# Layer 1 by list schedules with real and imaginary parts on the partitions, and the convolution passes' stores by Pool

## The chip, the cores and the metric

The kernel runs on one core of a Trainium2 chip. The metric is the device time of one execution in microseconds (us), of which the median of several is taken. The core has five engines: TensorE (PE; its weight loads are shown apart as PEld), VectorE (DVE), ScalarE (ACT), GpSimd (POOL) and SyncE (SP), which only issues DMAs here. ACT and POOL can issue DMAs too. All DMAs share 16 DMA engines. Everything is float32.

## The reference

A batch x of 8 images with 32 channels of 256x256 goes through four layers, each `x = x + layer(gn(x))`, where `gn` normalises groups of two channels. The change is in layers 0 and 1.

```python
# layer 0: two hyperbolic 3x3 convolutions
out = _hconv(x, w1, b1);  out = _hrelu(_hbn(out, g1, beta1))
out = _hconv(out, w2, b2); out = _hrelu(_hbn(out, g2, beta2))
# _hconv: u = logmap0(x); y = conv3x3(u) + b; project(expmap0(y))
# logmap0, expmap0 and project scale each pixel by a function of its norm over the channels
# layer 1 (xs = every second row and column; p, q of 4 poles; i, k channels)
alpha = fft2(xs)
inv1 = 1 / (wp1 - lam1);  inv2 = 1 / (wp2 - lam2)
t1   = einsum('biox,oikp->bikpx', alpha, inv1)
res1 = einsum('bikpx,xikq,ikpq->bkpq', t1, inv2, res)
e1 = exp(wp1 * y);  e2 = exp(wp2 * x)          # complex
tmp = einsum('abpq,bipz->abqiz', res1, e1)
x1  = real(einsum('abqiz,biqx->aizx', tmp, e2)) / (Sx * Sy)
```

Layer 2 (mixing in windows) and layer 3 (a binary pattern) are the longer half of the kernel and are not touched.

## The kernel before

Seven stages follow one another. Intermediate images lie in DRAM (`v1`, `v2`, `x1`, `x2`, `x3`).

- **first_pass** (L519) and **second_pass** (L613): the two convolutions. An image lies on the partitions as 4 bands of rows x 32 channels (`pad`, two buffers), and is worked on in 8 units of 8 rows. For each image first come the norms: squares on ACT (`square`), four 128x32 matmuls per unit that add them over channels (`norms`, L309), the scale factor on small tiles (`artanh_over`, `cut`), then 16 times a pair of matmuls that spreads the factor over the channels into PSUM tile `q`, of which there is one buffer (L348), and a DVE product into `pad` (L588 in the first pass). Then each unit is convolved (`convolution`, L373): 144 matmuls of 32x32 weights (L391), two ACT copies of PSUM into `u` (L405), squares, the norm (L416), `cut`, two spreads (L429) with products on DVE (L434), statistics, and four stores of 256 KB each to `v` (L451) on the SP queue. `u` has two buffers. The first pass also loads `pad` by 16 DMAs per image on the SP queue (L549) and takes group statistics of the image (`stats`, `combine`, with a `pow` on POOL).
- **third_pass** (L683): the end of layer 0, writes `x1`. Its stores are issued by POOL (L810).
- **laplace_forward** (L862): a setup computes `1/(wp - lam)` for both axes, times the DFT matrices, into `g1`, `g2a`, `g2b` (8 blocks of 1024 columns: DVE work, one square on POOL, 64 matmuls, copies). Then, for each of the 32 input channels: load `xs`; two DVE operations normalise it into `xn`; 8 matmuls of 256 columns into `pz`; a copy to `zs` shared by ACT and DVE; 64 matmuls of 128x32 weights and 8 columns into `pt` (L963); and four DVE operations that add `pt` times the residues to `acc`. The result `res` goes to DRAM (`scratch`).
- **laplace_inverse** (L983): `scratch` is read back (`r`), and with a mask becomes block diagonal weights `bd`. For each block of 4 channels, two complex exponentials are made from angles on DVE and sines on ACT. For each channel, `xt` (2 MB) is loaded; for each of 8 images: two matmuls of 128x128 weights and 512 columns accumulate into `pu` (L1059, from `ea` and `eb`: one complex product takes both, since only the 32x4 pairs of output channel and pole lie on the partitions), ACT copies to `us` (L1067), four matmuls of 128x128 and 256 columns into `po` (L1071), DVE adds to `xt` (L1074) and takes statistics (L1077). `xt` is stored on the SP queue.
- **row_norms** (L1082): group means and variances from those statistics. `rsqrt_col` (L233) takes a `pow` on POOL over 256 columns (L241).
- **mixing** (L1338) and **binary_pattern** (L1619): layers 2 and 3.

The order of work in both convolution passes is set by `Plan` (L120). Every step is given with its engine, an assumed duration (`took`), an assumed time until its result is there (`lag`), and how much earlier than its job it ranks (`lead`). `issue` simulates engines that take the ready step of the lowest rank, counts free buffers, and emits the instructions in that order. The hardware then runs each engine's list in order. `conv_pass` (L505) mixes the units of image b with the preparation of image b+1. Before the change, `laplace_forward` and `laplace_inverse` are plain loops that the tile framework orders by dependencies.

Of the kernel before, what the change touches and what calls it, by code (L numbers as in the profile page):

```python
# [32 lines left out]
P = 128  # L33
NB = 8
# [229 lines left out]
def flat(ap):  # L264
    return ap.rearrange("p a b -> p (a b)")
# [5 lines left out]
class Strip:  # L271
# [101 lines left out]
    def convolution(self, pad, b, k, w):  # L373
# [27 lines left out]
        u = Buf(self.work, [P, 4, FD], "u", 2)  # L401
# [19 lines left out]
        s = self.narrow("cut", 2)  # L421
# [26 lines left out]
        def store():  # L448
            for j in range(4):
                at = k * UN + j * FD  # L450
                nc.sync.dma_start(dst[:, :, at : at + FD], u[32 * j : 32 * j + 32])  # L451

        plan.add("SP", 1.2, store, [u], lag=6.0)
# [12 lines left out]
    def artanh_over(self, pn):  # L466

        nc, plan = self.cx.nc, self.plan
        ln, w, p, z = (self.narrow(x) for x in ("ln", "w", "p", "z"))
        f = self.narrow("f", 2)  # L470
# [6 lines left out]
        ts(ln, pn, NORM_EPS**2, None, ALU.max)  # L477
        act(ln, ln, AF.Ln)
        act(w, ln, AF.Exp, scale=0.5)
        act(f, ln, AF.Exp, scale=-0.5)  # L480
# [132 lines left out]
def second_pass(cx, v1, sb, v2):  # L613
# [5 lines left out]
    with (  # L619
# [9 lines left out]
        def prepare(b):  # L629
# [29 lines left out]
            def narrow():  # L659
                f = strip.narrow("f", 2)  # L660
                strip.cut(f, pn)
                times = lambda rows, pf: nc.vector.tensor_tensor(rows, rows, pf, ALU.mult)
                later.extend(strip.factors(pad, f, times))
# [198 lines left out]
def laplace_forward(cx, x1, norms, scratch):  # L862

    nc = cx.nc
    KP = NC * M1
    with (
        cx.tc.tile_pool(name="g", bufs=1) as gp,
        cx.tc.tile_pool(name="wl", bufs=2) as work,
    ):


        g1 = gp.tile([P, NC, 2, KP], F32, name="g1", tag="g1")
        g2a = gp.tile([P, NC * NC, 2, M2], F32, name="g2a", tag="g2a")
        g2b = gp.tile([P, NC * NC, 2, M2], F32, name="g2b", tag="g2b")
        cosm, sinm, nsinm = (cx.keep(n, gp) for n in ("dft_cos", "dft_sin", "dft_nsin"))
        freq = cx.keep("dft_freq", gp)
        with cx.tc.tile_pool(name="pg", bufs=2, space=PSUM) as psum:
            for axis, grid in ((0, "L1_conv_x_grid"), (1, "L1_conv_t_grid")):
                zg = gp.tile([P, 3], F32, name="zg", tag=f"zg{axis}")
                nc.sync.dma_start(zg[:], cx.ins[grid][:, 0:3].to_broadcast([P, 3]))  # L880
                lam = gp.tile([P, 1], F32, name="lam", tag=f"lam{axis}")
                nc.vector.tensor_tensor(lam[:], zg[:, 2:3], zg[:, 0:1], ALU.subtract)
                nc.vector.reciprocal(lam[:], lam[:])
                nc.vector.tensor_tensor(lam[:], lam[:], freq[:], ALU.mult)
                BL = 2 * FD
                for blk in range(NC * KP // BL):
                    cols = slice(blk * BL, (blk + 1) * BL)
                    wr = work.tile([P, BL], F32, name="wr", tag="wr")
                    wi = work.tile([P, BL], F32, name="wi", tag="wi")
                    for t, part in ((wr, "r"), (wi, "i")):  # L890
                        src = cx.ins[f"L1_conv_wp{axis + 1}{part}"].rearrange("(o i) k p -> o (i k p)", o=1)
                        nc.sync.dma_start(t[:], src[:, cols].to_broadcast([P, BL]))
                    den = work.tile([P, BL], F32, name="den", tag="den")
                    tmp = work.tile([P, BL], F32, name="tmp", tag="tmp")
                    nc.vector.tensor_scalar(wi[:], wi[:], lam[:], None, ALU.subtract)
                    nc.vector.tensor_tensor(den[:], wr[:], wr[:], ALU.mult)
                    nc.gpsimd.tensor_tensor(tmp[:], wi[:], wi[:], ALU.mult)
                    nc.vector.tensor_tensor(den[:], den[:], tmp[:], ALU.add)
                    nc.vector.reciprocal(den[:], den[:])
                    nc.vector.tensor_tensor(wr[:], wr[:], den[:], ALU.mult)  # L900
                    nc.vector.scalar_tensor_tensor(wi[:], wi[:], -1.0, den[:], ALU.mult, ALU.mult)
                    for h in range(BL // FD):
                        hc = slice(h * FD, (h + 1) * FD)
                        pg = psum.tile([P, 2, FD], F32, name="pg", tag="pg")
                        nc.tensor.matmul(pg[:, 0, :], cosm[:], wr[:, hc], start=True, stop=False)
                        nc.tensor.matmul(pg[:, 0, :], sinm[:], wi[:, hc], start=False, stop=True)
                        nc.tensor.matmul(pg[:, 1, :], cosm[:], wi[:, hc], start=True, stop=False)
                        nc.tensor.matmul(pg[:, 1, :], nsinm[:], wr[:, hc], start=False, stop=True)
                        lo = blk * BL + h * FD
                        if axis == 0:  # L910
                            i0 = lo // KP
                            for c in range(2):
                                nc.vector.tensor_copy(
                                    g1[:, i0 : i0 + FD // KP, c, :],
                                    pg[:, c, :].rearrange("p (i k) -> p i k", k=KP),
                                )
                        else:
                            k = slice(lo // M2, (lo + FD) // M2)
                            re, im = (pg[:, c, :].rearrange("p (k q) -> p k q", q=M2) for c in range(2))
                            nc.vector.tensor_copy(g2a[:, k, 0, :], re)  # L920
                            nc.vector.tensor_copy(g2a[:, k, 1, :], im)
                            nc.scalar.copy(g2b[:, k, 1, :], re)
                            nc.scalar.mul(g2b[:, k, 0, :], im, -1.0)

        acc = gp.tile([NB * M1, 2, NC, 2, M2], F32, name="racc", tag="racc")
        nc.vector.memset(acc[:], 0.0)
        with (
            cx.tc.tile_pool(name="pz", bufs=1, space=PSUM) as psz,
            cx.tc.tile_pool(name="pt", bufs=2, space=PSUM) as pst,
        ):  # L930
            for i in range(NC):
                xs = work.tile([P, NB, W], F32, name="xs", tag="xs")
                nc.sync.dma_start(xs[:], x1[:, i].rearrange("b (y t) w -> t y b w", t=2)[0])
                rr = work.tile([NB * M1, 2, NC * 2 * M2], F32, name="rr", tag="rr")
                nc.sync.dma_start(rr[:], cx.ins["res"][:, i])
                xn = work.tile([P, NB, SUB], F32, name="xn", tag="xn")
                nc.vector.tensor_tensor(
                    xn[:], xs[:, :, 0:W:2], norms[:, :, 0, i : i + 1].to_broadcast([P, NB, SUB]), ALU.mult
                )
                nc.vector.tensor_tensor(  # L940
                    xn[:], xn[:], norms[:, :, 1, i : i + 1].to_broadcast([P, NB, SUB]), ALU.add
                )
                pz = psz.tile([P, NB, 2 * KP], F32, name="pz", tag="pz")
                for b in range(NB):
                    nc.tensor.matmul(
                        pz[:, b, :],
                        xn[:, b, :],
                        g1[:, i].rearrange("p c k -> p (c k)"),
                        start=True,
                        stop=True,  # L950
                    )
                zs = work.tile([P, 2, NC, NB, M1], F32, name="zs", tag="zs")
                half = NB // 2
                zt = zs.rearrange("p c k b m -> p b (c k) m")
                zf = pz.rearrange("p b (c m) -> p b c m", m=M1)
                nc.scalar.copy(zt[:, :half], zf[:, :half])
                nc.vector.tensor_copy(zt[:, half:], zf[:, half:])
                pt = pst.tile([NB * M1, NC * 2 * M2], F32, name="pt", tag="pt")
                for k in range(NC):
                    o = pt[:, k * 2 * M2 : (k + 1) * 2 * M2]  # L960
                    ik = i * NC + k
                    for c, g2 in enumerate((g2a, g2b)):
                        nc.tensor.matmul(  # L963
                            o,
                            zs[:, c, k].rearrange("p b m -> p (b m)"),
                            g2[:, ik].rearrange("p c q -> p (c q)"),
                            start=c == 0,
                            stop=c == 1,
                        )
                for c in range(2):  # L970
# [8 lines left out]
        for c in range(2):  # L979
            nc.sync.dma_start(scratch[c], res[:, c].rearrange("p k q -> p (k q)"))  # L980


def laplace_inverse(cx, x1, scratch, x2):  # L983

    nc = cx.nc
    KP = NC * M1
    BL = 4
# [886 lines left out]
```

## Time and profile before

| what | value |
|---|---|
| time, median of 3 runs | 14024.65 us (14023.85 to 14066.98) |
| the profiled execution: its own time | 14021.73 us |
| its span | 14020.0 us |
| PE / PEld / DVE busy | 10705.7 / 4220.3 / 8731.4 us |
| ACT / POOL busy | 7714.0 / 166.6 us |
| DMA | 1834.96 MB, mean 131 GB/s |

All readings are from the one profiled execution. A line of a group reads: source line, engine, operation, output<-input with shapes, count, then busy us and mean ns of one, then idle time of that engine just before such instructions and what ended most of it. In tables by stretch, each engine's busy time is followed by its instruction count; PEclk is the granted TensorE clock (1 is full). "issue" as a releaser is time in which the engine waited for nothing that the profile shows.

### The profile page before, as it was taken

What the parts mean: (1) busy time and instruction counts of PE and PEld (TensorE: products, weight loads), DVE (VectorE), ACT (ScalarE), POOL (GpSimd) and SP (SyncE); (2) the same over time, 40 slices, a digit from 0 to 9 for tenths busy, and PEclk for the clock granted to TensorE, in tenths of its full rate; (3) what the DMA queues carried; (4) which work ended last, traced back from release to release, by engine and by line L of the source; (5) the groups of instructions that cost most, each with busy time, mean ns of one, the idle gap of its engine ahead of it and who ended that gap; (6) DMA issues with size and microseconds to landing.
All of it is one profiled execution on the core that took longest, in us unless ns stands there. A gap on an engine that the chain in (4) does not pass through costs nothing.

```text
span 14020.0 us, 359842 instructions
## 1 busy us (share of the span) xinstructions
PE 10705.7 (76%) x165700; PEld 4220.3 (30%) x165700; DVE 8731.4 (62%) x7524; ACT 7714.0 (55%) x6456; POOL 166.6 (1%) x340
## 2 busy tenths in 40 slices
PE   5877899974447899367887878878788788987666
PEld 1222233320016566122332323323232233322222
DVE  3544343344564554256787878878787788887555
ACT  2332444443310222366877778777777778775555
POOL 0000000000000000100000000000000000000000
PEclk8887889975557899588998989989899899998777
DMA  5344333345642244455566556655665565553444
GB/s 95 75 91 91 95 100 103 102 116 187 196 148 77 95 149 149 109 148 144 143 150 155 145 145 150 153 147 137 156 150 151 141 151 147 132 132 98 129 126 126
DMA packets 1562774, 1834.96 MB, mean 131 GB/s; under 512 B 634352, under 2 KB 1279536, under 8 KB 1495728
## 3 DMA queue, kind: packets, MB, share of 16 engines
q1 hardware_dynamic: 1527472, 1744.72, 47.9%
q0 software_dynamic: 33792, 67.21, 1.5%
q8 instruction: 1301, 21.32, 0.6%
q14 instruction: 209, 1.71, 0.0%
HBM read 1140.39 MB, written 671.12 MB: 129 GB/s over the span
## 4 chain that ended last, share of the span: by engine, by line
PE 15%; DVE 14%; DMA 11%; ACT 10%; SPq 5%; issue 4%; DVEq 0%; ACTq 0%; POOL 0%; POOLq 0%
PE acc L1276 10%; DVE en L1304 8%; DMA raw<-x 4%; ACT e L1250 4%; DMA yt<-y 3%; DMA xt<-x 3%; SPq L1381 2%; DVE xc L1237 2%; PE q L1196 2%; SPq L1701 1%; DVE s L1682 1%; ACT e L1294 1%; ACT xc L1213 1%; PE q L1221 1%; SPq L1384 1%
## 5 line engine op out<-in xcount | busy, mean ns | idle before, releaser
L1276 PE MATMUL acc<-en,k_kw 32*32 32x512 f32 x49152 | 2164.5, 626 | 492.1 <-DVE en L1304 454.3
L1304 DVE SCALAR_TENSOR_TENSOR en<-e,en 128x2048 f32<-128x2048 f32 x1024 | 2343.7, 2289 | 210.6 <-PE acc L1276 155.7
L1250 ACT ACTIVATE e<-xc,off 128x2048 f32<-128x2048 f32 x768 | 1515.0, 2008 | 569.2 <-DVE xc L1237 489.2
L1304 DVE SCALAR_TENSOR_TENSOR en<-e 128x2048 f32<-128x2048 f32 x512 | 1170.8, 2287 | 348.4 <-ACT e L1294 190.8
L1276 PEld LDWEIGHTS acc<-en,k_kw 32*32 32x32 f32 x49152 | 710.4, 105 | 1482.9 <-DVE en L1304 1009.7
L1276 PE MATMUL acc<-e,k_kw 32*32 32x512 f32 x16384 | 1036.2, 673 | 104.0 <-ACT e L1294 35.5
L1237 DVE TENSOR_TENSOR xc<-xc,q 128x1024 f32<-128x1024 f32 x640 | 751.0, 1215 | 489.8 <-PE q L1230 489.5
L1294 ACT ACTIVATE e<-e 128x2048 f32<-128x2048 f32 x512 | 970.3, 1924 | 1.5
L1682 DVE TENSOR_TENSOR s<-raw 128x2313 f32<-128x2313 f32 (+2 forms) x256 | 627.7, 2495 | 478.3 <-DMA raw<-x 478.3
L1668 PE MATMUL acc<-s,mats 32*32 32x512 f32 x16384 | 697.9, 728 | 231.9 <-ACT s L1685 223.1
L1685 ACT ACTIVATE s<-s,vecs 128x2313 f32<-128x2313 f32 (+2 forms) x256 | 554.4, 2170 | 553.7 <-DVE s L1682 553.7
L405 ACT ACTIVATE u<-acc,k_vec 128x1024 f32<-128x1024 f32 x256 | 270.8, 1108 | 1062.3 <-DMA v<-u 694.0
L391 PE MATMUL acc<-pad,wb 32*32 32x512 f32 x18432 | 736.9, 649 | 141.1 <-issue 131.8
L1213 ACT ACTIVATE lsq<-q 128x1024 f32<-128x1024 f32 x512 | 526.6, 1028 | 530.6 <-PE q L1196 468.1
L434 DVE TENSOR_TENSOR u<-u,q 128x1024 f32<-128x1024 f32 x256 | 312.4, 1220 | 738.6 <-PE q L429 547.7
L391 PE MATMUL acc<-pad,k_cw 32*32 32x512 f32 x18432 | 736.6, 625 | 15.7 <-ACT u L405 10.8
L711 PE MATMUL n<-sq,k_gather 128*32 128x512 f32 x1024 | 243.7, 1045 | 439.6 <-ACT sq L729 438.2
L1276 PE MATMUL acc<-sg,k_kws 128*32 128x512 f32 x4096 | 504.5, 636 | 47.9 <-DVE sg L1335 40.6
L1196 PE MATMUL q<-yt,k_center 32*32 32x512 f32 x4096 | 313.2, 722 | 284.3 <-DMA yt<-y 227.8
L1213 ACT ACTIVATE xc<-q 128x1024 f32<-128x1024 f32 x512 | 529.3, 1034 | 0.0
L348 PE MATMUL q<-f,k_spread 32*128 32x512 f32 x1024 | 392.8, 853 | 173.2 <-DVE pad L588 93.0
L1071 PE MATMUL po<-ea,us 128*128 128x256 f32 x2048 | 506.5, 391 | 1.2 <-ACT us L1067 1.2
(291 smaller groups left out, 15967.4 us busy)
## 6 DMA issues: line engine op xcount, KB each, us to landing
v<-u SPq DMA_DIRECT2D x512, 256.0 KB
xt<-x SPq DMA_DIRECT2D x128, 1024.0 KB
pad<-v SPq DMA_DIRECT2D x64, 1024.0 KB
v<-v SPq DMA_DIRECT2D x64, 1024.0 KB
xt<-in_x SPq DMA_DIRECT2D x64, 1024.0 KB
x<-xt POOLq DMA_DIRECT2D x64, 1024.0 KB, 38.8
xt<-x SPq DMA_DIRECT2D x32, 2048.0 KB
x<-xt SPq DMA_DIRECT2D x32, 2048.0 KB
```

The source lines that it names most:

```text
L391: nc.tensor.matmul(acc[i // 2][32 * j : 32 * j + 32, i % 2, :], w[rows, tap, :], pad[rows, r : r + 2, dx : dx + W], start=tap == 0, stop=t ...
L1071: nc.tensor.matmul(po[:, t, :], us[:, c, t:W:2], ex[:, j, c, :], start=c == 0, stop=c == 1)
L1196: nc.tensor.matmul(pc[32 * j : 32 * j + 32, t, :], center[rows, :], src[rows, j * FD : (j + 1) * FD], start=True, stop=True,)
L1213: lambda pc=pc, h=h, fn=fn, out=out: nc.scalar.activation(half(out, h), flat(pc.get()), fn, bias=bias),
L1237: lambda pr=pr, h=h: nc.vector.tensor_tensor(half(xc, h), half(xc, h), flat(pr.get()), ALU.mult),
L1250: nc.scalar.activation(es[d][:], xs[:].rearrange("p i n -> p (i n)"), AF.Exp if exp else AF.Square, bias=kan.off[:, d : d + 1], scale=2.0 ...
L1276: nc.tensor.matmul(acc[bank][32 * to : 32 * to + 32, :], w[rows, out] if w.shape[-1] == P else w[rows, :], rhs[rows, cols] if rhs.shape[-1 ...
L1294: plan.add("ACT", 1.91, lambda: nc.scalar.activation(es[d][:], es[d][:], AF.Exp, scale=-1.0), [], [es[d]])
L1304: lambda: nc.vector.scalar_tensor_tensor(n[:], es[-1][:], BIG, prev[:], ALU.min, ALU.mult),
L1668: nc.tensor.matmul(acc[i][32 * j : 32 * j + 32, :], mats[part, m, part], rhs[part, 2 * j : 2 * j + 2, :], start=m == 0, stop=m == len(weig ...
L1682: nc.vector.tensor_tensor(d, raw[:, r0 + dy : R + 1 + dy, c0 + dx : c1 + dx], raw[:, r0 : R + 1, c0:c1], ALU.subtract)
L1685: nc.scalar.activation(d, d, AF.Sigmoid, scale=vecs[:, 0, b : b + 1])
```

## The change

Four parts.

**Convolution passes.** `u` gets a third buffer, and the stores of `v` go from the SP queue to the POOL queue; the plan gets 4.0 and 12.0 us for them in place of 1.2 and 6.0. To make room, the narrow tiles `cut` and `f` go from two buffers to one, and `ln` and `w` share one tile.

```diff
-        u = Buf(self.work, [P, 4, FD], "u", 2)
+        u = Buf(self.work, [P, 4, FD], "u", 3)
...
-        s = self.narrow("cut", 2)
+        s = self.narrow("cut")
...
-                nc.sync.dma_start(dst[:, :, at : at + FD], u[32 * j : 32 * j + 32])
-
-        plan.add("SP", 1.2, store, [u], lag=6.0)
+                nc.gpsimd.dma_start(dst[:, :, at : at + FD], u[32 * j : 32 * j + 32])
+
+        plan.add("POOL", 4.0, store, [u], lag=12.0)
...
-        ln, w, p, z = (self.narrow(x) for x in ("ln", "w", "p", "z"))
-        f = self.narrow("f", 2)
+        w, p, z, f = (self.narrow(x) for x in ("w", "p", "z", "f"))
```

**laplace_forward** is written as steps of a `Plan`. In the setup both squares and the copies to `g1` go to ACT, and one pool of PSUM tiles serves setup and channels. Per channel, `xn` is made by 8 ACT operations (scale and bias in one) instead of 2 DVE operations. `pt` is made by 16 matmuls with 128x128 weights and 32 columns instead of 64 with 128x32 weights and 8 columns: four k at once, of whose products only the diagonal blocks are used. `pt`, `rr`, `acc` and `res` so have 128 partitions instead of 32, and `res` leaves by 8 DMAs on SP and ACT instead of 2.

```diff
+                for k in range(0, NC, 4):
                     for c, g2 in enumerate((g2a, g2b)):
                         nc.tensor.matmul(
-                            o,
-                            zs[:, c, k].rearrange("p b m -> p (b m)"),
-                            g2[:, ik].rearrange("p c q -> p (c q)"),
+                            pt[:, k * 2 * M2 : (k + 4) * 2 * M2],
+                            zs[:, c, k : k + 4].rearrange("p k b m -> p (k b m)"),
+                            g2[:, i * NC + k : i * NC + k + 4].rearrange("p k c q -> p (k c q)"),
                             start=c == 0,
                             stop=c == 1,
                         )
```

**laplace_inverse** is a `Plan` too. Real and imaginary parts of the first exponential lie together on the partitions (64 pairs of channel and pole each, in two halves `h`), so that `pu` is two matmuls of 128x64 weights, each into its own half of the partitions, with no accumulation. There are three exponentials per block instead of two (`ea`, `eb`, `ex`), with the quarter turns given by a constant `phase`. `xt` has three buffers, `pu` and `po` four each, and `x2` is stored by POOL.

```diff
+                def rows(b=b, pu=pu):
+                    for h, e in enumerate((ea, eb)):
                         nc.tensor.matmul(
-                            flat(pu),
-                            bd[:, c, b].rearrange("p k q -> p (k q)"),
+                            flat(pu.get())[64 * h : 64 * h + 64, :],
+                            bd[:, h, b].rearrange("p k q -> p (k q)"),
                             e[:, j].rearrange("p c w -> p (c w)"),
-                            start=c == 0,
-                            stop=c == 1,
+                            start=True,
+                            stop=True,
                         )
...
+                plan.add("PE", 1.0, rows, [ea, eb], [pu], lead=0.5)
+                plan.add("ACT", 0.6, lambda pu=pu, us=us: nc.scalar.copy(us[:], pu[:]), [pu], [us], lead=0.5)
...
+                plan.add("PE", 1.75, columns, [us, ex], [po])
...
+                "POOL", 1.5, lambda: nc.gpsimd.dma_start(x2[:, i].rearrange("b (y t) w -> y b (t w)", t=2), xt[:]),
+                [xt], lag=14.0,
```

`scratch` is read back by 32 DMAs on SP and ACT instead of 16 on SP. In the order that the plan makes, TensorE does the 8 pairs of a channel in a row, then 8 times the four matmuls of L1071.

**row_norms** picks out each partition's own channel (`own`) before the `pow`, which so works on 8 columns instead of 256.

```diff
-    rsqrt_col(cx, f2(rs), f2(v), GN_EPS, "r")
+    own(m, mv[:, 0, :])
+    own(v, mv[:, 1, :])
+    rs = pool.tile([P, NB], F32, name="rn_rs", tag="rn_rs")
+    rsqrt_col(cx, rs[:], mv[:, 1, :], GN_EPS, "r")
```

## The prediction

> **What bounds the kernel now.** I read the table by stretch first, cut at the stages (start:end, length, then busy us of PE, PEld, DVE, ACT, POOL, then PEclk, DMA share, GB/s).
>
> ```profile
> 0.00:1656.00 1656.00, 1229.45 (x20544) 425.55 (x20544) 755.39 (x1008) 487.87 (x425) 15.13 (x61) 0.83 0.41 84
> 1656.00:3023.00 1367.00, 1203.51 (x20516) 404.31 (x20516) 532.76 (x603) 605.74 (x472) 6.41 (x26) 0.88 0.37 101
> 3023.00:4100.00 1077.00, 483.78 (x1572) 93.29 (x1572) 550.59 (x641) 415.56 (x248) 50.37 (x82) 0.51 0.58 188
> 4100.00:4256.00 156.00, 77.67 (x145) 33.28 (x145) 129.25 (x115) 8.68 (x16) 19.34 (x8) 0.71 0.26 84
> 4256.00:4694.00 438.00, 357.57 (x4608) 315.09 (x4608) 152.75 (x222) 32.38 (x32) 0.00 (x0) 0.72 0.25 73
> 4694.00:4730.00 36.00, 0.00 (x0) 0.00 (x0) 15.60 (x36) 7.75 (x12) 0.00 (x0) 0.50 0.42 130
> 4730.00:5651.00 921.00, 918.22 (x3072) 579.25 (x3072) 481.17 (x717) 254.02 (x385) 0.00 (x0) 1.00 0.42 139
> 5651.00:5703.00 52.00, 1.86 (x4) 0.80 (x4) 8.75 (x25) 0.00 (x0) 41.24 (x1) 0.53 0.12 41
> ```
>
> They are: first pass, second pass, third pass (unchanged), setup of the forward transform, its 32 channels, start of the inverse, its 32 channels, row norms. TensorE is busy without a gap in the inverse (918 of 921, clock 1.00): only less TensorE work shortens it. The setup is DVE's, the row norms POOL's. In the convolution passes TensorE waits for a fifth and an eighth of the time. The waits (total us, times, longest) and the timeline of 500 to 600 say for what, in the first pass:
>
> ```profile
> ACT u L405 <- DMA v<-u: 557.8, 31, 43.8
> ...
> PE acc L391 <- issue: 131.8, 7, 22.4
> ```
> ```profile
> 499.72 19.39 SPq L549 DMA_DIRECT2D pad<-in_x  x7
> ...
> 508.36 2.07 PE L348 MATMUL q<-f,k_spread 32*128 32x512 f32 x4 [1.39 <-DVE pad L588]
> ...
> 519.22 5.23 SPq L451 DMA_DIRECT2D v<-u  x4
> ...
> 534.73 2.12 ACT L405 ACTIVATE u<-acc,k_vec 128x1024 f32<-128x1024 f32 x2 [43.65 <-DMA v<-u]
> ...
> 535.94 6.07 PE L391 MATMUL acc<-pad,wb 32*32 32x512 f32 x96 [22.04 <-issue]
> ...
> 566.54 1.06 PE L416 MATMUL n<-sq,k_gather 128*32 128x512 f32 x8
> ...
> 567.53 3.41 PE L391 MATMUL acc<-pad,wb 32*32 32x512 f32 x96
> ```
>
> The SP queue issues the next image's loads up to 519; only then the store whose landing frees a `u`. ACT waits 43.65 us for it, and TensorE 22.04 behind ACT. This comes once per image (7 times, 131.8). Besides, spreads into the single `q` that stand back to back run at DVE's pace: starts 3.46 us apart (504.90, 508.36), against 1.06 where other matmuls lie between.
>
> **The change part by part.** *Convolution passes.* I rebuilt the period of an image, L405 to L405 (534.7 to 730.1 = 195.4 us). A unit alone takes 14.28 (L405 at 2950.02, 2964.29, 2978.57, where no preparation is left); 8 of them + 16 spreads at 1.06 + 8 norms at 1.0 + 1.3 = 140.5. Each back-to-back spread adds 2.4. The order of TensorE's instructions before has 14 of these per image in the first pass: 140.5 + 34 + the 22 of idle time = 196; in the second 10: 164, measured 164.1. So the model holds. After the change the order has 10 and 4: 164.5 and 150, if the store wait goes too. It should: the stores leave from a queue with nothing of SP's in it, and even if one landed as late as now, a third `u` gives a unit's grace (14.28 bare, some 20 with preparation) against 22. Gain: 31.5 in each of six periods' worth (first and last image count as one together) = **190**; in the second 14.4 x 6 = **86**. Bounds: 60 (rival B) to 55.5 x 6 = 333 for the first pass (all above bare work), nothing to 142 for the second.
>
> The new waits: on POOL, four issues per unit. The nearest row is the third pass's store, of 1 MB, four times as large: L810 0.68 us in the median, 0.887 at most, so at most 2.7 us per unit of some 20. Queued behind them are the `pow` of the statistics, which is late by one unit's stores at worst (2.7 x 7 images = 19 if nothing hides it), and `clear`, which waits for TensorE anyway. Behind the `pow` the next stores wait for DVE; rival B prices that. The narrow tiles' single buffers are shared by steps that follow one another on ACT and DVE anyway; I take nothing, the 14.4 or 31.5 of a period is at stake.
>
> *Setup, 156 us, DVE.* The copies to `g1` (16 x 0.675) and the eight squares (1.316) leave DVE (21.3); 7 of waiting for POOL's squares and 5 of two channels' `xn` go too: **33**. ACT (8.68 busy) hides them.
>
> *Forward channels, 438 / 32 = 13.7 us each.* TensorE is late in `pt` and waits for DVE:
>
> ```profile
> L963 PE MATMUL pt<-g2a,zs 128*32 128x8 f32 x2048 | 176.8, 189 | 78.3 <-DVE zs L957 78.3
> ```
>
> That wait is 2.5 us per channel, and the clock is 0.72. After: `pz` has 8 x 256 columns, which at the inverse's rate (2048 columns in 3.60 us) take 3.6. `pt`: neighbouring records of L963 start 0.063 us apart in pairs at full clock, 0.031 for a load of 32 columns; a load of 128 taken at four times that, 32 records (two per matmul) = 4.0 (bounds: 1.25 by columns alone, 5 by L1071's 0.196 loads half hidden). With channels overlapped by the plan, `zs` is no longer waited for, and I take clock 1.0 as in the inverse, which also has no waits: 7.6 x 32 + 6 = 249, a gain of **189**. ACT has 8 x about 0.2 + 1.2, DVE 1.2 + 4 x 0.4: both below 7.6. Bounds: 214 (one `xs` load landed 6.7 us after issue) and 349 (7.6 at clock 0.72, and start).
>
> *Start of the inverse, 36 us.* Two more angles per block chain of DVE (six of 3.95 = 23.7), twice as many loads of `r` on two queues, and the same round trip by DRAM (some 9): about 54, a loss of **18**.
>
> *Inverse, 921 / 256 = 3.60 us per image.*
>
> ```profile
> L1071 PE MATMUL po<-ea,us 128*128 128x256 f32 x2048 | 506.5, 391 | 1.2 <-ACT us L1067 1.2
> L1059 PE MATMUL pu<-ea,bd 128*128 128x512 f32 x512 | 263.4, 596 | 38.6 <-DVE ea L1042 38.6
> L1059 PE MATMUL pu<-eb,bd 128*128 128x512 f32 x512 | 262.5, 594 | 0.0
> ...
> L1074 DVE SCALAR_TENSOR_TENSOR xt<-po,xt 128x512 f32<-128x512 f32 x256 | 176.5, 690 | 430.8 <-PE po L1071 430.7
> ```
>
> L1059 and L1071 stream 1024 columns each, 1.80 us each. L1071 stays. L1059 becomes two matmuls of 64 weight columns into different column halves. No row shows such a pair. Nearest is L416: four 128x32 matmuls of 512 columns, one per column quarter, from 566.54 to 567.53 = 0.99 us, little over one stream of 512 (0.90), so they run side by side. I take 0.99; bounds 0.90 and 1.80 (rival A). Per channel 8 x 0.99 + 8 x 1.80 = 22.3; x 32 = 714, a gain of **207**. The others fit: DVE 8 x 1.38 (L1074 + L1077) + a quarter of a block's exponentials (31.1) = 18.9 of 22.3; ACT some 262 in all; DMA 4 MB in 22.3 us, 190 GB/s, against 188 in the third pass's mean.
>
> The Trainium skill, "TensorEngine Tiling (Array Packing)", section "Key Properties", says that changing the tiling mode drains TensorE. L416 stands between 32x32 matmuls, so by that rule its 0.09 above 0.90 is the price of going in and out; the changed order does eight pairs in a row, and would pay it once per channel: 32 x (7.2 + 0.09 + 14.4) = 694 instead of 714, an estimate 20 us below the forecast.
>
> *Row norms.* The `pow` took 41.24 us for 256 columns, so about 1.3 for 8; the picking is two small operations earlier instead of later: 52 becomes 13, a gain of **39**. DVE and everything else wait for it now, so all of it counts.
>
> *Sum.* 190 + 86 + 33 + 189 - 18 + 207 + 39 = 726. From the profiled execution's own 14021.7 (span 14020.0): 13296. The median of the runs shown lies 3 higher: **13300**.
>
> **The rivals.** *A: the halves don't run side by side.* Then the pair costs 1.80 and the inverse stays at 921; the change doesn't do what it says there. Against: L416's 0.99. For: those are quarters, and 64-column halves have no row. 13300 + 207 = 13507.
>
> *B: DVE takes the place of the store.* The pad loads (starting 496.64, all DMA engines full to 545) are still what is late: the statistics wait for them in DVE's queue (68.7 us in all before), and behind them wait `cut` and the products that TensorE needs, and behind the `pow` the stores. Loads that no longer wait between stores also meet them in the DMA engines. Then the first pass gains 60 and the second nothing: 13300 + 216 = 13516. Both A and B: 13723.
>
> *C, slower: POOL's issue of stores.* 32 per image are in order with the rest of POOL. At 0.68 they take 22 us of 165; but if each took t, the period is at least 32 t. Layer 1 gains 450 by the terms above, so the kernel ends beyond 0.3% slower only if both passes together (3023 now, 236 of it at their ends) take 492 more: 3279 / 16 = 205 per image, t = 6.4 us, 9.4 times the row. At 7 us: 16 x 224 + 236 = 3820, and 14372 in all. The Trainium skill, "SBUF — State Buffer", in its "DVE blocks DMA" trap, has a cause for it: a DMA from the POOL queue has its descriptors written by GpSimd, which a DVE instruction holding the shared port locks out. The trace speaks against it: with DVE busy 551 of 1077 us in the third pass, no L810 took over 0.887.
>
> **How the numbers follow.** Forecast 0.68, A 0.10, B 0.15, A with B 0.04, C 0.03. Low end: forward 35 less, inverse 24 less, and the passes half way to bare work (100 less): 13150. High end: A and B lie inside, B with 30 of its own: 13550; A with B and C are left out. A clock that stays at 0.72 in the forward channels (13400) is inside. A measurement of this kernel tells 0.3% (42 us) from no change. Faster 0.95 (all but C and a part of what is not thought of), same 0.02, slower 0.03.
>
> **What would show it.** In the changed profile: no wait of L405 for `v<-u` over a few us and periods of some 164 and 150 us (else B); `rows` pairs about 1 us apart (1.8: A); PEclk near 1.0 and some 7.7 us per channel in the forward transform; POOL's store issues under 0.9 us (6: C); a `pow` of 2 us. The prediction is wrong if the store wait turns into a wait for loads, if the halves run one after another, or if DVE (18.9 of 22.3 by my count) becomes the bound of the inverse.

## The result and the profile after

The changed kernel takes 13422.83 us (median of 4 runs, 13402.61 to 13439.57) against 14024.25 before: ratio 0.9565, 95% interval 0.9541 to 0.9588, some 600 us less. The profiled execution took 13415.47, its span 13413.7. The time lies inside the range on record and 123 us above the forecast.

By stage, each from its first instruction to that of the next one, in the profiled executions (us):

| stage | before | after | change | forecast |
|---|---|---|---|---|
| first pass | 1656.3 | 1540.3 | -116 | -190 |
| second pass | 1366.3 | 1311.3 | -55 | -86 |
| third pass (unchanged) | 1078.8 | 1093.9 | +15 | 0 |
| forward: setup | 154.5 | 138.9 | -16 | -33 |
| forward: channels | 437.3 | 237.0 | -200 | -189 |
| inverse: start | 37.2 | 55.6 | +18 | +18 |
| inverse: channels | 920.9 | 679.4 | -242 | -207 |
| row norms | 51.9 | 11.9 | -40 | -39 |
| mixing and binary pattern (unchanged) | 8316.6 | 8345.3 | +29 | 0 |

So layer 1 gave more than forecast (479 against 450), the passes less (171 against 276), and 44 us came back in stages that nobody touched. The surplus of layer 1 hides a part of what the passes fell short by, so the total lies nearer to the forecast than the passes do. The table by stretch of the profile after, with the same columns as before (the line from 3945.50 is the forward setup):

```profile
0.00:1540.30 1540.30, 1221.54 (x20544) 417.04 (x20544) 751.61 (x1008) 487.29 (x425) 154.40 (x315) 0.88 0.43 92
1540.30:2851.60 1311.30, 1143.37 (x20516) 389.42 (x20516) 532.30 (x602) 602.25 (x472) 145.63 (x283) 0.91 0.36 103
...
3945.50:4084.40 138.90, 77.02 (x144) 33.24 (x145) 99.27 (x85) 39.10 (x62) 0.00 (x0) 0.70 0.31 96
4084.40:4321.40 237.00, 234.25 (x1537) 216.57 (x1535) 85.85 (x162) 127.32 (x274) 0.00 (x0) 0.96 0.53 158
...
4377.00:5056.40 679.40, 677.58 (x3072) 470.78 (x3072) 533.75 (x853) 239.56 (x396) 27.62 (x32) 1.00 0.55 186
5056.40:5068.30 11.90, 1.92 (x4) 0.80 (x4) 8.32 (x26) 0.00 (x0) 2.49 (x2) 0.63 0.48 176
```

Read the PE column against the length. The forward channels (234 of 237, clock 0.96) and the inverse (678 of 679) are now TensorE's without a gap, with DVE well below. In the passes TensorE still has 319 and 168 us without a matmul.

The store wait has nearly gone. From the waits of ACT in the first pass, and from the page of the store's line (ns: least, median, most):

```profile
ACT u L405 <- DMA v<-u: 69.1, 8, 11.3
```
```profile
L451 POOL DMA_DIRECT2D v<-u x512: 550/550/754, 207.5 to 2852.5; - x171
```

557.8 us of waiting became 69.1, and an issue on POOL takes 0.55 us, a twelfth of what rival C needed. But in the middle of the passes the periods of an image are 177 to 182 us in the first and 160 in the second, not 164.5 and 150.

### The profile page after: what moved, and what is told of

Same layout as the page of the kernel before. It is cut to its first block, busy times and chain, and to the rows that moved or that the text cites. A ratio compares the mean times of both kernels' runs of the same rounds, so it can differ in the third digit from the quotient of the medians.

```text
span 13413.7 us, 354346 instructions
## 1 busy us (share of the span) xinstructions
PE 10274.0 (77%) x162628; PEld 3991.5 (30%) x162628; DVE 8696.2 (65%) x7604; ACT 7824.6 (58%) x6762; POOL 415.7 (3%) x876
## 4 chain that ended last, share of the span: by engine, by line
PE 16%; DVE 15%; DMA 12%; ACT 10%; SPq 5%; issue 4%; DVEq 0%; ACTq 0%; POOL 0%; POOLq 0%
PE acc L1392 10%; DVE en L1420 9%; DMA raw<-x 4%; DMA yt<-y 4%; ACT e L1366 3%; SPq L1497 3%; DMA xt<-x 2%; DVE xc L1353 2%; PE q L1312 2%; SPq L1817 1%; DVE s L1798 1%; PE q L1337 1%; PE q L1346 1%; ACT xc L1329 1%; ACT st L1446 1%
## 5 line engine op out<-in xcount | busy, mean ns | idle before, releaser
L1337 PE MATMUL q<-lsq,k_gather 128*32 128x512 f32 x2560 | 457.5, 662 | 57.7 <-ACT xc L1329 57.0
L1784 PEld LDWEIGHTS acc<-s,mats 32*32 32x32 f32 x16384 | 302.5, 114 | 650.6 <-ACT s L1801 447.0
```

The lines of the kernel that those rows point to most:

```text
L1337: nc.tensor.matmul(pn[32 * i : 32 * i + 32, 0, :], gather[:], sq[:, i, :], start=True, stop=True)
L1784: nc.tensor.matmul(acc[i][32 * j : 32 * j + 32, :], mats[part, m, part], rhs[part, 2 * j : 2 * j + 2, :], start=m == 0, stop=m == len(weig ...
```

## The experiments

All times are medians beside the kernel before on the same chip; its median was 14034 beside the first four runs, 14040 beside the next four, 14038 beside the last. Stage times are from each run's one profile.

| kernel | us | ratio (interval) | first | second | inverse | three unchanged stages |
|---|---|---|---|---|---|---|
| conv_only | 13880.2 | 0.9882 (0.9861 to 0.9903) | 1533.0 | 1317.6 | 919.5 | 9422 |
| layer1_only | 13574.6 | 0.9664 (0.9644 to 0.9685) | 1652.3 | 1362.8 | 679.4 | 9436 |
| store_on_sp | 13446.3 | 0.9567 (0.9542 to 0.9593) | 1600.2 | 1278.8 | 678.1 | 9439 |
| u_two | 13552.7 | 0.9651 (0.9626 to 0.9676) | 1573.7 | 1413.3 | 679.3 | 9426 |
| edges_told | 13365.9 | 0.9521 (0.9503 to 0.9540) | 1538.4 | 1256.3 | 679.3 | 9466 |
| pool_first_sp_second | 13373.1 | 0.9523 (0.9499 to 0.9546) | 1545.1 | 1278.4 | 679.2 | 9420 |
| pairs_alternate | 13462.8 | 0.9585 (0.9564 to 0.9606) | 1539.0 | 1311.1 | 711.1 | 9461 |
| halves_apart | 13550.1 | 0.9646 (0.9626 to 0.9666) | 1539.8 | 1311.0 | 802.3 | 9456 |
| told_sp_second | 13366.2 | 0.9519 (0.9505 to 0.9533) | 1536.9 | 1268.3 | 679.2 | 9426 |
| cut_two | 13430.4 | 0.9565 (0.9549 to 0.9580) | 1560.5 | 1284.4 | 679.3 | 9452 |
| after_again | 13417.2 | 0.9556 (0.9542 to 0.9570) | 1537.8 | 1313.9 | 678.5 | 9434 |
| before_again | 14041.3 (one run) | | 1655.8 | 1367.7 | 920.3 | 9413 |

**One part alone: conv_only, layer1_only.** The first is the kernel before with the passes' edits, the second the changed kernel with those edits undone.

> The kernel before with the convolution passes' part of the change alone (three u, stores by POOL, narrow tiles shared); layer 1 and the row norms as before. In the changed kernel's profile the first pass ends 116 us and the second 55 us earlier, and the third pass, in which nothing is changed, is 15 us longer. Theory 1: the passes' gain stands alone and the third pass's 15 us are a scatter from run to run: 171 less, 13853. Rival: the 15 us come with the change of the passes and show here again: 13868, third pass near 1087.

> The changed kernel with the convolution passes as before (two u, stores on SP). By the changed kernel's profile layer 1 and the row norms gain 479 us: 13545 if nothing else moves. Theory 1: the 28 us by which mixing and the binary pattern (unchanged) were longer are scatter and go or come here by chance, between 13530 and 13575. Rival: they come with the change of layer 1 (where x2 is written from, what lies in the queues): 13573, mixing near 7128 and the binary pattern near 1217 again.

The parts add: 154 and 460 against the kernel before, 614 together, where the whole gave 601 in its own comparison. The totals can't tell the theories apart. By the stages both rivals' values came: the third pass took 1090.8 in conv_only (rival: 1087), and mixing and the binary pattern took 7129.5 and 1214.8 in layer1_only (rival: 7128 and 1217). But the third pass is as long in layer1_only (1091.7), whose passes are those of before, so its 15 us don't need the change of the passes; and mixing took 7121.2 in conv_only, whose layer 1 is that of before, against 7109.9. What two more profiles of the same kernels say stands at the end of this section.

**Queue and third tile: store_on_sp, u_two.**

```diff
# store_on_sp
-                nc.gpsimd.dma_start(dst[:, :, at : at + FD], u[32 * j : 32 * j + 32])
+                nc.sync.dma_start(dst[:, :, at : at + FD], u[32 * j : 32 * j + 32])
-        plan.add("POOL", 4.0, store, [u], lag=12.0)
+        plan.add("SP", 1.2, store, [u], lag=6.0)
# u_two
-        u = Buf(self.work, [P, 4, FD], "u", 3)
+        u = Buf(self.work, [P, 4, FD], "u", 2)
```

> The changed kernel with the stores of v back on the SP queue (with the plan's old 1.2 and 6.0), three u kept. Theory 1: the third u covers a store that comes late behind the loads, as the prediction argued (a unit's grace against 22 us), so the passes are within 20 us of the changed kernel: 13420 to 13445. Rival: the queue is what matters; a store behind 16 loads stays late by more than a unit, the first pass loses 10 us or more per image, 70 to 116 in all: 13495 to 13540.

> The changed kernel with two u instead of three, stores by POOL kept. Stores by POOL landed 4.5 us after issue in the median. Theory 1: the queue alone would do: within 20 us of the changed kernel, 13420 to 13445. Rival: the third u is needed, because while the next image's loads hold the DMA engines a store takes as long as before: ACT waits for v<-u again once per image, 10 to 20 us each: 13500 to 13550.

With before and after they make a table of two by two (the narrow tiles are shared in all but before). First pass: 1656 with neither, 1574 by the queue alone, 1600 by the tile alone, 1540 with both. Second pass: 1366, 1413, 1279, 1311. In the first pass both are needed for the whole gain. The waits of ACT there are, with stores on SP, then with two u:

```profile
ACT u L405 <- DMA v<-u: 249.5, 31, 24.2
```
```profile
ACT u L405 <- DMA v<-u: 75.0, 12, 7.8
```

Without the queue the store is still up to 24.2 us late with three tiles, and TensorE waits 57.0 us behind ACT's copies to `u` (8.2 in the changed kernel), most of the 60 that the first pass is longer. So the prediction's second argument (a third tile covers it even on SP) was too kind: a unit's grace falls short. The total of store_on_sp fell near theory 1's band only because the second pass got better by 33. There the move to POOL, with the durations that the plan is told for it, costs time, which no term had. In u_two the third tile's worth is 33 and 102; the rival's sum was right within 3 us, its reason (a store as late as before) was not, as ACT waits at most 7.8. What the third tile gives is mostly the order. In TensorE's timelines an image in the middle of a pass has 14 and 11 back-to-back spreads in u_two, nearly as before (14 and 10); with three tiles it has 10 and 4, and 12 and 4 with the stores on SP. Over a whole pass that is 76 against 52 in the first and 116 against 67 in the second; at the prediction's 2.4 us each, an estimate, 58 and 118, somewhat above the 33 and 102.

**What the second pass lost: edges_told.** The timeline of the changed kernel at the end of an image (start, length, engine, line, and in brackets the wait):

```profile
2222.13 15.46 SPq L638 DMA_DIRECT2D pad<-v  x4
...
2247.23 0.82 ACT L667 ACTIVATE pad<-pad,bsb 128x512 f32<-128x512 f32 x1 [23.36 <-DMA pad<-v]
2247.96 2.08 ACT L653 ACTIVATE pad<-pad,bsb 128x2048 f32<-128x2048 f32 x1
2249.94 0.61 ACT L463 ACTIVATE cut<-cut 128x512 f32<-128x512 f32 x1
2250.59 0.63 ACT L464 ACTIVATE cut<-cut 128x512 f32<-128x512 f32 x1
...
2251.27 2.08 PE L429 MATMUL q<-cut,k_spread 32*128 32x512 f32 x4 [11.45 <-ACT cut L464]
```

ACT stands 23.36 us at L667, which needs the edge rows of the next image. They are issued behind eight loads of 1 MB. The cut, which only waits for ACT, is queued behind it, and TensorE waits 11.45 for the cut. The plan believed that the edges land 5 us after issue and that a load takes 0.4. ACT stood at these loads before the change too, for 133.1 us in the second pass, but TensorE hardly waited for a cut then. The kernel before, waits in the second pass:

```profile
ACT pad L668 <- DMA pad<-v: 133.1, 7, 21.1
...
PE q L429 <- ACT cut L464: 10.9, 10, 2.2
```

So the wait isn't new; what is new is that the order puts the cut behind it. The edit tells the plan otherwise; every DMA stays in its place, and one ACT instruction per image moves.

```diff
-                plan.add("SP", 0.8, edges, [(pad, "border")], [(pad, "edge")], lag=5.0)
+                plan.add("SP", 0.8, edges, [(pad, "border")], [(pad, "edge")], lag=27.0)
```

> The changed kernel; in the second pass the plan is told that the two edge loads of an image take 27 us to land instead of 5. The order of all DMAs stays; on ACT one instruction per image moves, the first operation on the edges (L667), some places later. Theory 1: in the changed kernel it waits 23 us for those loads, with the cut's logarithm and exponential queued behind it, for which TensorE waits 11.5 us, six times (most of 82.5): the second pass loses 60 to 70 us, 13350 to 13365. Rival: TensorE's next work waits for the loads anyway, and the wait moves to the next square or edge spread: within 15 us of the changed kernel.

TensorE's waits in the second pass, changed kernel first, then edges_told:

```profile
PE q L429 <- ACT cut L464: 82.5, 14, 11.9
```
```profile
PE q L429 <- ACT cut L464: 15.2, 8, 2.2
```

The second pass lost 55 us and the periods became 149.8 to 150.2: the forecast's 150. Theory 1 holds, with 55 us instead of the 60 to 70 that it gave.

**Can the passes be better: pool_first_sp_second, told_sp_second, cut_two.** The first lets the second pass store on SP, the next adds edges_told to it, the last gives `cut` two buffers again.

> The changed kernel with the stores on POOL in the first pass and on SP in the second, three u in both. Theory 1: the queue matters where loads of 16 pieces lie on SP (first pass: 60 us by the run with all stores on SP) and costs in the second pass only by the order that its durations make (33 us better on SP there): first pass 1540, second 1279, 13390. Rival: the second pass's gain on SP was tied to its own start from a first pass by SP: 13420 or more.

> Stores by POOL in the first pass and by SP in the second, and the plan told 27 us for the edge loads. Theory 1: both edits of the second pass remove the same wait of TensorE behind the edges, so the two don't add: second pass 1255 to 1280, 13350 to 13375. Rival: they add (33 and 55): second pass near 1223, 13330.

> The changed kernel with two buffers for the narrow tile cut again (f and w stay at one). The prediction took nothing for the single buffers. Theory 1: they cost little; the waits of TensorE for the cut (25 us in the first pass) come from the order on ACT, and the sum of both passes stays within 15 us of the changed kernel's 2852. Rival: the single buffer delays the next unit's cut, and with two both passes together gain 30 us or more.

Store by POOL in the first pass and by SP in the second: as expected, 1278.4. Told as well: 1268.3; the two edits don't add, since both take away the same wait (in store_on_sp TensorE waits for the cut once in the second pass, 2.2 us). edges_told (13365.9) and told_sp_second (13366.2) beat both kernels; they and pool_first_sp_second (13373.1) can't be told from each other. cut_two put 20 us into the first pass and took 27 out of the second. Its total stays within theory 1's 15 us (2844.9 against 2851.6), but by two changes that cancel, which theory 1 didn't have. Most of these edits also reorder the plan's lists, so the price of a buffer isn't seen alone.

**The pair of halves: pairs_alternate, halves_apart.**

```diff
# pairs_alternate
-                plan.add("PE", 1.0, rows, [ea, eb], [pu], lead=0.5)
-                plan.add("ACT", 0.6, lambda pu=pu, us=us: nc.scalar.copy(us[:], pu[:]), [pu], [us], lead=0.5)
+                plan.add("PE", 1.0, rows, [ea, eb], [pu])
+                plan.add("ACT", 0.6, lambda pu=pu, us=us: nc.scalar.copy(us[:], pu[:]), [pu], [us])
# halves_apart: rows of four images in one step
+                        for h, e in enumerate((ea, eb)):
+                            for n in range(b, b + 4):
...
-                plan.add("PE", 1.0, rows, [ea, eb], [pu], lead=0.5)
+                    plan.add("PE", 4.0, rows, [ea, eb], [x[0] for x in bufs[b : b + 4]], lead=0.5)
```

> The changed kernel with each pair of 128x64 matmuls followed by the four 128x128 ones of an image instead of eight pairs in a row. In the changed kernel eight pairs take 7.0 us and eight groups of four 14.1, without a gap. Theory 1: changing between the two shapes costs about 0.09 us per in and out, as L416's 0.99 against 0.90 suggests: 7 more per channel, 7 x 32 x 0.09 = 20 us: inverse 700, 13443. Rival: it costs nothing: inverse 679 to 683.

> The changed kernel with the pairs taken by fours: the four matmuls of the first half one after another, then the four of the second half. Only the one at the border has a neighbour in the other half. Theory 1: the two halves run side by side only as neighbours: 7 streams of 0.88 instead of 4, 2 x 3 x 0.88 = 5.3 us more per channel, 168 more in all: inverse 847, 13590. Rival: a matmul of 64 weight columns costs half of one with 128 by itself, whatever stands beside it: inverse within 10 us of 679.

One stretch of TensorE's timeline in each: changed kernel, pairs_alternate, halves_apart (two records per matmul).

```profile
4704.35 14.09 PE L1164 MATMUL po<-e,us 128*128 128x256 f32 x64
4718.37 7.09 PE L1150 MATMUL pu<-e,bd 128*64 128x512 f32 x32
4725.39 4.81 PE L1164 MATMUL po<-e,us 128*128 128x256 f32 x21
```
```profile
4701.44 1.94 PE L1150 MATMUL pu<-e,bd 128*64 128x512 f32 x8
4703.31 3.73 PE L1164 MATMUL po<-e,us 128*128 128x256 f32 x16
4706.97 1.94 PE L1150 MATMUL pu<-e,bd 128*64 128x512 f32 x8
```
```profile
4703.41 3.73 PE L1170 MATMUL po<-e,us 128*128 128x256 f32 x16
4707.07 5.42 PE L1156 MATMUL pu<-e,bd 128*64 128x512 f32 x16
4712.42 9.77 PE L1170 MATMUL po<-e,us 128*128 128x256 f32 x44
```

Eight pairs start to end in 4725.39 - 4718.37 = 7.02 us, 0.88 per pair: one stream's time for two matmuls. With the halves apart, four pairs take 5.35 (4712.42 - 4707.07) instead of 3.5, and the inverse 123 us more, so the order decides, not the weight columns: theory 1. Its size was 168; the single records in that stretch start 0.43 apart, and sixteen of them fill twelve places and not the fourteen I counted, so the second half sets in while two matmuls of the first are still to come. Alternating costs 32 us, more than the 20 expected: two images take 5.53 us (4706.97 - 4701.44), where bare streams are 2 x (0.86 + 1.73) = 5.17, so 0.36 per in and out. The edit doesn't alternate at every image as its expectation says: the plan takes pairs by twos to fours, and TensorE goes in and out 100 times, against 34 in the changed kernel. 66 more at 0.36 are 24 us, and TensorE waits 7.4 for `us`; so the expectation had over three times too many changes at a quarter of the price.

**The same kernels again: before_again, after_again.**

> The kernel before, once more. The profiles of this case with unchanged code show the third pass between 1079 and 1105 us, mixing between 7110 and 7158, the binary pattern between 1204 and 1220. Theory 1: that is scatter between executions and chips, and this profile lies inside these spans away from the first one (third pass over 1079, mixing over 7110). Rival: the first profile's low values belong to the kernel before: third pass 1079, mixing 7110, binary pattern 1207 again, within 4 us each.

> The changed kernel once more, beside the two that follow. First pass 1540, second 1311, inverse 679, each within 3 us, total 13400 to 13440 by both theories; the third pass and mixing anywhere in their spans by theory 1 (scatter), at 1094 and 7128 by the rival.

The third pass (1078.8 and 1086.4 in the two profiles of before, 1093.9 and 1107.3 in those of the changed kernel) and the binary pattern (1206.7 and 1214.9, 1217.3 and 1214.0) moved between profiles of the same kernel by 3 to 13 us; mixing gave 7109.9 and 7111.5 before, 7128.0 and 7112.4 after. So after_again speaks for scatter and against its rival (1094 and 7128 again), while before_again lies between: its third pass and binary pattern moved, its mixing did not. The last column of the table says the rest: 9395 in the first profile, 9413 in the second, up to 9466 elsewhere. Both of before are the lowest, so a part of some 20 us may belong to the changes of layer 1 or of the passes. I can't name a mechanism, and leave that open.

## Why the prediction was right, and where it was wrong

**Store wait:** right that it goes (557.8 to 69.1), and that POOL's issue is cheap (0.55 us). The reason needs both edits, as the two by two shows, and the third tile works mostly through the order of the spreads: the prediction counted that order rightly (10 and 4) but gave the tile only the wait to cover.

**First pass, forecast -190, got -116: the term 140.5 of "bare work" failed.** Per period the forecast had 140.5 + 24. In the changed profile (image from 864.6 to 1041.3) I subtracted from each group of matmuls its time in an undisturbed stretch. The spreads cost 25.5, as forecast. The rest came out 10 to 12 longer: convolution matmuls behind a stretch of waits run slower (5 to 10 per image), and the statistics' matmuls (2) were not counted. TensorE's timeline shows it:

```profile
871.11 2.08 PE L429 MATMUL q<-cut,k_spread 32*128 32x512 f32 x4 [1.58 <-DVE pad L587]
873.12 5.56 PE L391 MATMUL acc<-pad,wb 32*32 32x512 f32 x96
...
886.36 3.41 PE L391 MATMUL acc<-pad,wb 32*32 32x512 f32 x96
```

The same 96 records take 5.56 behind the waits and 3.41 in the flow. The granted clock (third number from the right) says why:

```profile
861.03:864.44 3.41, 0.97 (x6) 0.30 (x4) 3.41 (x6) 0.00 (x0) 0.00 (x0) 1.00 1.08 302
864.45:878.08 13.63, 10.06 (x107) 2.99 (x104) 12.44 (x18) 4.03 (x3) 0.00 (x0) 0.50 1.13 196
878.10:895.15 17.05, 13.47 (x243) 4.15 (x216) 12.14 (x17) 5.29 (x5) 2.17 (x4) 1.00 0.49 104
```

It is halved from 864.44 to 878.09, and over the image its mean is 0.88. The 140.5 of the prediction took every matmul in it at full speed.

The model had met 196 in the kernel before because two errors cancelled there: by the same subtraction the spreads cost 30 and not 34, and the rest was 5 too small. A sum that fits one kernel doesn't vouch for its parts. The Trainium skill, "TensorE: Matmul & The Clock Gate", Part 1, has full rate return after some 3.4 us of steady work; here TensorE worked without a wait from 871.11, and full clock came 7.0 us later, about twice that. It has the rate fall after an idle window of about that length; here no single wait in that stretch was over 2.5 us, and TensorE was busy for 0.97 of the last 3.41 us before the fall. So short waits in a row were enough.

**Second pass, forecast -86, got -55:** the order's count was right (periods of 150 once the wait is gone). The store wait went there too (136.2 before). What failed is that the forecast put nothing in its place: the new order has the cut behind ACT's wait for the edge loads, a wait of rival B's kind on ACT instead of DVE, which costs 11.5 us of TensorE per image. The line of that wait stood in the profile before, where it cost TensorE next to nothing.

**Setup, -33, got -16:** DVE's busy time fell as forecast (129 to 99), but what is late next was not looked for. DVE waits for loads of the poles, 11.9 us and 4.9 us, where the profile before has 2.4 in all:

```profile
DVE wi L904 <- DMA wi<-in_L_conv_wp1i: 11.9, 1, 11.9
```

**Forward channels, -189, got -200:** right in mechanism and nearly in size. L999 now waits 1.5 us for `zs` in all, and a channel takes 7.4 (forecast 7.6); `pz` streams in 3.5 as taken, `pt` in 3.5 instead of 4.0.

```profile
L999 PE MATMUL pt<-g2a,zs 128*128 128x32 f32 x512 | 97.8, 273 | 1.5 <-DVE zs L990 1.5
```

**Inverse, -207, got -242:** right that the halves run side by side; rival A falls. Mis-sized were the 0.99 per pair (0.88) and the 1.80 for the columns: before, each image went from one kind of matmul to the other and back, and of its 3.60 only 4 x 0.429 + 8 x 0.216 = 3.44 were streaming. That 0.15 x 256 = 38 us left with the new order. The Trainium skill's rule in "TensorEngine Tiling (Array Packing)", "Key Properties", that a change of tiling mode drains TensorE, points the right way: an in and out between 128x64 and 128x128 costs 0.36 against 0.15 between two shapes of one mode, and paying it once per channel is why eight pairs in a row are good. The estimate by it, 694, was the nearer one to 679, in part by luck: it took 0.09 for an in and out.

**Start of the inverse and row norms:** as forecast (+18; the `pow` now 1.7 us). **Unchanged stages:** taken at nothing, 44 us longer in the profile. Two profiles of the kernel before differ by 18 there; how much of the rest is scatter is not shown.

## What to carry to other kernels

A list schedule is as good as the durations that it is told: look in the profile for an engine that waits for a DMA which the plan thought landed, and see what is queued behind it; here one number was worth 55 us. A buffer more can be worth more through the order that it allows than through the wait that it covers: count both. Test a model of a stage term by term on the trace, not by its sum. Matmuls of half the weight columns pay in full when the two halves are neighbours in the order, and kinds of matmul are better done in long runs.

## What the runs showed of the hardware

Two matmuls of 128x64 weights into different halves of the partitions take one's time (0.88 us for a pair of 512 columns in float32); with four of one half before four of the other they still overlap for two of the four. The granted clock fell to half in a stretch where no wait was over 2.5 us, with TensorE busy for 0.97 of the last 3.41 us, and the same 96 convolution records then took 5.56 us and not 3.41. A change between 128x64 and 128x128 and back costs 0.36 us, between 512 and 256 columns of 128x128 weights 0.15. The three stages with unchanged code took 9395 to 9466 us in fourteen profiles of twelve kernels, 0.8%; alone, the third pass spread by 2.8% (1078.8 to 1108.9), mixing by 0.7% (7109.9 to 7157.7) and the binary pattern by 1.4% (1203.5 to 1220.1). A smaller difference of such a stage between two single profiles says nothing.
